# Recurrence of a gated layer: four lanes of image pairs with staggered entry, input scaled in the step's addition, one-step transfers

## The chip, the cores and the metric

The kernel runs on one core of one Trainium2 chip. The metric is device time in microseconds for one execution of the whole program, and the median of several runs is what counts. All data are fp32 in device memory.

## The reference, cut to what matters

The whole network is a 2-D LSTM over 16 images of 64 x 64 tokens with 128 channels, then an attention layer, then a feed-forward layer with a recurrence over the tokens. The change lies in that last part alone:

```python
Wx = einsum('bti,hi->bth', x, W)                    # x: 16 images, 4096 tokens, 128 channels
mean, var = mean(flat), var(flat)                   # over all images and tokens, per channel
Wx = (flat - mean) * rsqrt(var + eps) * gamma + beta
def step(yt, wx_t):
    yt = sigmoid(wx_t + yt @ V.T)
    return yt, yt
_, ys = scan(step, zeros, Wx over the tokens)
t = t + ys
```

The mean and variance need all of Wx, so the recurrence cannot begin before the attention stage has written its last piece of Wx.

## The kernel before, in words

`group_stats`, `lstm_grid`, `landmarks` and `attention` run first. `attention` leaves three things: `wx` in device memory (per image, 128 channels on the partitions by 4096 tokens, before the normalisation), `wx_stats` (its statistics per 512 tokens) and `t2` (the sum that the recurrence's output is added to, tokens by channels).

`recurrence` (L985) works as follows. The 4096 tokens of an image are cut into 128 chunks (CH) of 32 tokens (L). All 128 chunks advance at once, one token per step, so that a step of an image pair (a group, GI = 2) is one tile of 128 channels x 256 columns. Since a chunk does not know the state at its start, 12 warm-up steps (WARM) over the last 12 tokens of the chunk before it produce it; at the end the state so found is compared with the true last state of the chunk before (L1110, L1111), and if any differs too much, `in_order` recomputes everything, which does not happen in the runs shown.

There are eight groups. FLIGHT = 4 of them are in flight together, so there are two rounds (L1097). A round is:

- `begin` (L1031): for each group, four loads of 1 MB of `wx` (L1041) into `rc_w` [channel, 64 chunks, 32 tokens] with three buffers. Each is normalised (x scale + shift) and turned from chunk-major to token-major order on the way, by 16 instructions of 512 columns a group: on GpSimd (POOL, L1050), and in the first round by turns on ScalarE (ACT, L1048). The result, `rc_ws`, holds eight tokens a tile, each as 256 packed columns.
- `warm` (L1064): 12 times over the four groups: a product with V on TensorE (PE, L1061), an addition on VectorE (DVE, L1073) and a sigmoid on ACT (L1074). The first has no product (L1071).
- `step` (L1077): 32 times over the four groups: product, addition in place (L1079), sigmoid in place (L1080).
- `store` (L1083): after each eighth step, for each group: a load of 1 MB of `t2` (L1088), 16 transposes of 128 x 128 on PE (L1093), added into the `t2` tile on DVE by fours (L1094), and a 1 MB store to the output (L1095).

The order on the engines comes from the program's order and a scheduler here; on the queue of SP (SyncE), which issues all the transfers, loads and stores wait for each other's buffers in the order in which they stand. The chunk-major tile, 32 tokens of 4 bytes per chunk, puts one token of neighbouring chunks 128 bytes apart.

Of the kernel before, what the change touches and what calls it, by code (L numbers as in the profile page):

```python
# [8 lines left out]
F32 = mybir.dt.float32  # L9
AF = mybir.ActivationFunctionType  # L10
ALU = mybir.AluOpType
AX = mybir.AxisListType
# [3 lines left out]
P = 128  # L16
# [968 lines left out]
def recurrence(nc, tc, wx, wx_stats, t2, ffn_v, gamma, beta, ident, mhalf, out):  # L985
# [2 lines left out]

    B, H, N = wx.shape
    CH = P
    L = N // CH
    S = 8
    NB = L // S
    GI = 2
    FLIGHT = 4
    WARM = 12
    AGREE = 2.0 ** -18
    NG = B // GI  # L1000
    W = GI * CH
    with ExitStack() as ctx:
        cp = ctx.enter_context(tc.tile_pool(name="rc_c", bufs=1))
        vT = cp.tile([P, P], F32, name="rc_vT")
# [1 line left out]
        shift = cp.tile([P, 1], F32, name="rc_shift")  # L1006
        res = cp.tile([P, NG], F32, name="rc_res")
        with ExitStack() as fast:
            lx = fast.enter_context(tc.tile_pool(name="rc_lx", bufs=3))
            wsp = fast.enter_context(tc.tile_pool(name="rc_wsp", bufs=FLIGHT * NB))  # L1010
            tp = fast.enter_context(tc.tile_pool(name="rc_tp", bufs=4))
            st = fast.enter_context(tc.tile_pool(name="rc_st", bufs=FLIGHT))
            ps_z = fast.enter_context(tc.tile_pool(name="rc_psz", bufs=4, space=PSUM))
            ps_t = fast.enter_context(tc.tile_pool(name="rc_pst", bufs=4, space=PSUM))

            v = cp.tile([P, P], F32, name="rc_v")
            nc.sync.dma_start(out=v, in_=ffn_v)
            vp = ps_t.tile([P, 4, P], F32, tag="t", name="rc_t")
            nc.tensor.transpose(vp[:, 0, :], v, ident)
            nc.vector.tensor_copy(vT, vp[:, 0, :])  # L1020
            mv = cp.tile([P, 2], F32, name="rc_mv")
            nc.vector.bn_aggr(mv, wx_stats.rearrange("p c s -> p (c s)"))
            inv_std(nc, cp, scale, mv[:, 1:2], mhalf, "rc")
            nc.vector.tensor_mul(scale, scale, gamma)
            nc.vector.tensor_mul(shift, mv[:, 0:1], scale)
            nc.vector.tensor_sub(shift, beta, shift)

            class Group:
                pass

            def begin(g):  # L1031
                gr = Group()
                gr.g = g
                gr.ws = [
                    wsp.tile([P, S, GI, CH], F32, tag="ws", name="rc_ws") for _ in range(NB)
                ]
                half = N // 2
                for i in range(GI):
                    for h in range(2):
                        w = lx.tile([P, CH // 2, L], F32, tag="w", name="rc_w")  # L1040
                        nc.sync.dma_start(  # L1041
                            out=w.rearrange("p c l -> p (c l)"), in_=wx[g * GI + i, :, h * half : (h + 1) * half]
                        )
                        for k in reversed(range(NB)):
                            src = w[:, :, k * S : (k + 1) * S].rearrange("p c s -> p s c")
                            dst = gr.ws[k][:, :, i, h * CH // 2 : (h + 1) * CH // 2]
                            if g < FLIGHT and (k + h) % 2:
                                nc.scalar.activation(dst, src, AF.Identity, bias=shift, scale=scale)  # L1048
                            else:
                                nc.gpsimd.tensor_scalar(dst, src, scale, shift, ALU.mult, ALU.add)  # L1050
                gr.a = st.tile([P, GI, CH], F32, tag="a", name="rc_a")
                gr.b = st.tile([P, GI, CH], F32, tag="b", name="rc_b")
                gr.y0 = st.tile([P, GI, CH], F32, tag="y0", name="rc_y0")
                for t in (gr.a, gr.b, gr.y0):
                    nc.vector.memset(t[:, :, 0:1], 0.0)
                gr.last = None
                return gr

            def product(gr):
                z = ps_z.tile([P, GI, CH], F32, tag="z", name="rc_z")  # L1060
                nc.tensor.matmul(z, vT, gr.last, start=True, stop=True)  # L1061
                return z

            def warm(gr, n):  # L1064

                s = L - WARM + n
                w = gr.ws[s // S][:, s % S, :, 0 : CH - 1]
                y = gr.y0 if n == WARM - 1 else (gr.a, gr.b)[n % 2]
                to = y[:, :, 1:CH]
                if gr.last is None:  # L1070
                    nc.scalar.activation(to, w, AF.Sigmoid)  # L1071
                else:
                    nc.vector.tensor_add(to, product(gr)[:, :, 1:CH], w)  # L1073
                    nc.scalar.activation(to, to, AF.Sigmoid)  # L1074
                gr.last = y

            def step(gr, s):  # L1077
                y = gr.ws[s // S][:, s % S]
                nc.vector.tensor_add(y, product(gr), y)  # L1079
                nc.scalar.activation(y, y, AF.Sigmoid)  # L1080
                gr.last = y

            def store(gr, k):  # L1083

                rows = slice(k * S, (k + 1) * S)
                bs = slice(gr.g * GI, (gr.g + 1) * GI)
                tt = tp.tile([P, GI, S, H], F32, tag="tt", name="rc_tt")
                nc.sync.dma_start(out=tt, in_=t2[bs].rearrange("b (c l) f -> c b l f", l=L)[:, :, rows, :])  # L1088
                for s in range(0, S, 2):
                    yp = ps_t.tile([P, GI, 2, P], F32, tag="t", name="rc_t")  # L1090
                    for i in range(GI):
                        for j in range(2):
                            nc.tensor.transpose(yp[:, i, j, :], gr.ws[k][:, s + j, i, :], ident)  # L1093
                    nc.vector.tensor_add(tt[:, :, s : s + 2, :], yp, tt[:, :, s : s + 2, :])  # L1094
                nc.sync.dma_start(out=out[bs].rearrange("b (c l) f -> c b l f", l=L)[:, :, rows, :], in_=tt)  # L1095

            for g0 in range(0, NG, FLIGHT):  # L1097
                groups = [begin(g) for g in range(g0, min(g0 + FLIGHT, NG))]
                for n in range(WARM):
                    for gr in groups:  # L1100
                        warm(gr, n)
                for s in range(L):
                    for gr in groups:
                        step(gr, s)
                    if s % S == S - 1:
                        for gr in groups:
                            store(gr, s // S)
                for gr in groups:
                    d = gr.a[:, :, 1:CH]
                    nc.vector.tensor_sub(d, gr.y0[:, :, 1:CH], gr.last[:, :, 0 : CH - 1])  # L1110
                    nc.vector.tensor_reduce(  # L1111
                        res[:, gr.g : gr.g + 1], d, AX.XY, ALU.max, apply_absolute_value=True
                    )

        worst = cp.tile([P, 1], F32, name="rc_worst")
        nc.vector.tensor_reduce(worst, res, AX.X, ALU.max)
# [121 lines left out]
```

## Time and profile before

| | us |
|---|---|
| median of 3 runs | 4762.01 (4759.21 to 4768.78) |
| the profiled execution's own time | 4758.9 |
| its span, first to last instruction | 4757.4 |
| first load of `rc_w` issued | 4392.8 |
| first sigmoid of the recurrence (L1071) | 4411.3 |
| last state of the first round added (L1079) | 4554.6 |
| first warm-up sigmoid of the last group of round two (L1071) | 4631.4 |
| last state of the second round added (L1079) | 4737.9 |

Over the span the page gives PE 92% busy, DVE 64%, ACT 51% and POOL 56%. These are means over stages with different limits: the first 4390 us are the LSTM and the attention, which the change does not touch. In a line on a group, the columns are the line of the program, the engine, the operation, the tile written and those read, the count, and the shortest, median and longest duration in ns; in a line by stage, they are the stretch in us, then busy time and number of instructions per engine. PEld is PE's loading of weights, which overlaps its products.

### The profile page before, as it was taken

The numbers are of one execution on the slowest core, as the hardware profiler recorded it, in microseconds if no ns is written. First come the engines' busy times: TensorE is split into PE (matmuls) and PEld (weight loads), VectorE is DVE, ScalarE is ACT, GpSimd is POOL, SyncE is SP. The second block draws the span as 40 slices with busy tenths as digits, with TensorE's granted clock in tenths as the row PEclk, the third lists the DMA queues.
The fourth block names the chain that finished last, engine by engine and source line by source line (L and its number), as shares of the span: only waits on it lengthen the run. The fifth ranks groups of instructions, "written<-read, shape, count | busy, mean of one in ns | idle before, by whom it ended". The sixth has DMA issues, their size and how long they took to land. (4 is left out here: it accounts for less than half of the span.)

```text
span 4757.4 us, 102456 instructions
## 1 busy us (share of the span) xinstructions
PE 4368.4 (92%) x39990; PEld 2791.1 (59%) x39990; DVE 3032.8 (64%) x6844; ACT 2438.7 (51%) x4467; POOL 2654.1 (56%) x3587
## 2 busy tenths in 40 slices
PE   7999999999997897899999999999999999986648
PEld 5867655556766894555555555555555555542537
DVE  7777777777776564456665656665566556544549
ACT  0666555556664223455555555555555555532725
POOL 0777777777776000566566656666656666653450
PEclk9999999999997798999999999999999999988769
DMA  7222222323321002122222222222222221111776
GB/s 293 62 76 77 78 76 79 81 78 85 83 70 34 3 14 62 34 56 59 59 57 56 57 63 56 58 58 60 57 57 58 59 58 54 49 47 56 288 295 248
DMA packets 403063, 386.50 MB, mean 81 GB/s; under 512 B 29712, under 2 KB 363408, under 8 KB 396176
## 3 DMA queue, kind: packets, MB, share of 16 engines
q1 hardware_dynamic: 402576, 379.90, 26.1%
q8 instruction: 319, 5.23, 0.5%
q14 instruction: 168, 1.38, 0.1%
HBM read 207.30 MB, written 172.63 MB: 80 GB/s over the span
## 5 line engine op out<-in xcount | busy, mean ns | idle before, releaser
L196 ACT ACTIVATE ls_g<-ls_z,ls_b 128x304 f32<-128x304 f32 (+26 forms) x950 | 508.7, 548 | 370.5 <-PE ls_z L194 334.0
L737 POOL TENSOR_TENSOR at_total<-at_total,at_e 128x512 f32<-128x512 f32 x480 | 610.7, 1272 | 60.5 <-ACT at_e L711 31.6
L190 PE MATMUL ls_z<-ls_xn,ls_w 128*128 128x304 f32 (+26 forms) x1900 | 610.2, 469 | 8.2 <-DMA ls_w<-in_L_conv_wf_dram 5.1
L24 POOL TENSOR_SCALAR at_ve<-at_mu 128x4 f32<-128x4 f32 x128 | 29.3, 229 | 885.4 <-DVE at_mu L866 885.4
L190 PEld LDWEIGHTS ls_z<-ls_xn,ls_w 128*128 128x128 f32 x1900 | 340.8, 196 | 184.5 <-issue 84.0
L668 DVE TENSOR_REDUCE at_mxq<-at_twin 128x2 f32<-128x1024 f32 x256 | 302.2, 1222 | 223.0 <-PE at_twin L664 223.0
L628 POOL TENSOR_SCALAR at_T<-at_T,at_nb 128x128 f32<-128x128 f32 x512 | 400.9, 795 | 13.3
L194 PE MATMUL ls_z<-ls_hsum,ls_u 128*128 128x304 f32 (+26 forms) x1140 | 371.2, 463 | 0.0
L893 ACT COPY at_fx<-at_bank 128x512 f32<-128x512 f32 x128 | 74.9, 585 | 566.8 <-DVE wx_stats L891 368.6
L711 ACT ACTIVATE at_e<-at_twin 128x1024 f32<-128x1024 f32 x256 | 263.5, 1032 | 186.5 <-PE at_twin L703 186.5
L837 DVE STREAM_TRANSPOSE at_dT<-at_twin 128x512 f32<-128x512 f32 x128 | 91.8, 717 | 395.3 <-PE at_twin L834 395.3
L276 POOL TENSOR_TENSOR ls_g<-ls_g,ls_cell 128x304 f32<-128x304 f32 (+26 forms) x190 | 175.9, 926 | 278.7 <-ACT ls_g L196 255.4
L799 DVE TENSOR_REDUCE at_top<-at_twin 128x16 f32<-128x1024 f32 x256 | 310.3, 1212 | 2.0 <-PE at_twin L791 2.0
L194 PEld LDWEIGHTS ls_z<-ls_hsum,ls_u 128*128 128x128 f32 x1140 | 213.4, 196 | 128.6 <-issue 78.2
L876 ACT ACTIVATE at_z<-at_u,at_nb,at_r 128x128 f32<-128x128 f32 x512 | 210.8, 482 | 135.3 <-POOL at_nb L871 135.2
L823 ACT ACTIVATE at_eT<-at_twin 128x1024 f32<-128x1024 f32 x256 | 247.7, 1019 | 52.2 <-PE at_twin L818 52.1
L233 ACT ACTIVATE ls_tt<-ls_tt,ls_nb 128x128 f32<-128x128 f32 (+9 forms) x632 | 261.0, 478 | 4.1 <-POOL ls_nb L228 4.1
L194 PE MATMUL ls_z<-ls_h,ls_u 128*128 128x304 f32 (+26 forms) x760 | 259.6, 465 | 2.3 <-DVE ls_h L284 2.1
L224 POOL TENSOR_TENSOR ls_tt<-ls_ve,mhalf 128x4 f32<-128x4 f32 (+2 forms) x190 | 228.7, 1203 | 15.2
L277 DVE TENSOR_TENSOR ls_g<-ls_g,ls_g 128x304 f32<-128x304 f32 (+26 forms) x190 | 98.4, 518 | 194.4 <-POOL ls_g L276 193.2
L225 POOL TENSOR_TENSOR ls_tt<-ls_ve,mhalf 128x4 f32<-128x4 f32 (+2 forms) x190 | 214.5, 1129 | 0.0
L194 PEld LDWEIGHTS ls_z<-ls_h,ls_u 128*128 128x128 f32 x760 | 142.4, 196 | 91.4 <-issue 50.9
(242 smaller groups left out, 10213.1 us busy)
## 6 DMA issues: line engine op xcount, KB each, us to landing
t<-ls_tt SPq DMA_DIRECT2D x392, 130.0 KB
at_T<-t SPq DMA_DIRECT2D x128, 264.0 KB
gs_xb<-in_x_dram SPq DMA_DIRECT2D x16, 2048.0 KB
at_xh<-t SPq DMA_DIRECT2D x128, 256.0 KB
t<-at_u SPq DMA_DIRECT2D x128, 256.0 KB
wx<-at_fx SPq DMA_DIRECT2D x128, 256.0 KB
rc_w<-wx SPq DMA_DIRECT2D x32, 1024.0 KB
rc_tt<-t SPq DMA_DIRECT2D x32, 1024.0 KB
```

What stands on the lines that cost most here:

```text
L190: nc.tensor.matmul(v.z[g][:, : v.cols], wt[g], v.xn, start=True, stop=False)
L194: nc.tensor.matmul(view(v, v.z[g]), ut[g], hin, start=False, stop=True)
L196: nc.scalar.activation(a[:, : v.cols], v.z[g][:, : v.cols], AF.Tanh if g == 4 else AF.Sigmoid, bias=bt[g])
L224: nc.gpsimd.tensor_tensor(v.tt[:, 0:k, F + 2], ve[:, 0, :k], mhalf[:, :k], ALU.pow)
L225: nc.gpsimd.tensor_tensor(v.tt[:, 0:k, F + 3], ve[:, 1, :k], mhalf[:, :k], ALU.pow)
L233: nc.scalar.activation(v.tt[:q, k, F + 4 :], v.tt[:q, k, 0:F], AF.Identity, bias=v.nb[:q, k : k + 1], scale=v.tt[:q, k, F + 3 : F + 4],)
L628: nc.gpsimd.tensor_scalar(x[:, c, :], x[:, c, :], nb[:, 0, c : c + 1], nb[:, 1, c : c + 1], ALU.mult, ALU.subtract)
L668: nc.vector.tensor_reduce(gr.im.mxq[:, 2 * i : 2 * i + 2, gr.g], s[i], AX.X, ALU.max)
L711: nc.scalar.activation(gr.e[:, 2 * i : 2 * i + 2].rearrange("p n c m -> p (n c m)"), gr.s[i].rearrange("p n m -> p (n m)"), AF.Exp)
L737: nc.gpsimd.tensor_tensor(total, total, e[:, :, c, :], ALU.add)
L799: nc.vector.tensor_reduce(gr.top[:, 2 * i : 2 * i + 2, 0:2, :].rearrange("p n j c -> p n c j"), gr.s[i].rearrange("p n (c j m) -> p n c j ...
L823: nc.scalar.activation(gr.eT[:, 2 * i : 2 * i + 2].rearrange("p n t -> p (n t)"), s[i].rearrange("p n t -> p (n t)"), AF.Exp)
```

## The change

`recurrence` alone is changed.

- The two rounds become four lanes. Lane g takes group g and then group g + 4; it enters nine steps (APART) after the lane before it, and its second group starts 45 steps after its first. The loop runs over 117 time slots. In each slot every live lane first issues its product, then its addition and sigmoid, then its transposes, in an order written out by hand for PE, DVE, ACT and POOL.
- The tile `rc_w` [channel, image, chunk, 32 tokens] holds a whole group, five such tiles exist, and the states overwrite the inputs in place. There is no token-major copy: the addition, the sigmoid, the product and the transposes of a main step all read or write columns that lie 128 bytes apart. Warm-up states still go to packed tiles, while their inputs are read from `rc_w`.
- The scaling moves into the step: the addition is a scalar_tensor_tensor (input x scale + product) with `scale` as a per-channel pointer, and the shift becomes the sigmoid's bias, a pointer as well. POOL has no work in the steps.
- `wx` comes in eight pieces of 512 KB a group, one a slot (the first two groups at once, in slot 0). `t2` and the output move in pieces of four steps, 512 KB each, with 2 KB runs in device memory (4 KB before); a `t2` piece is asked for three slots ahead of its first step. Each pair of steps is turned and added as soon as it is done.

```diff
@@ -988,17 +988,22 @@
 
 
 
+
+
     B, H, N = wx.shape
     CH = P
     L = N // CH
-    S = 8
+    S = 4
+    AHEAD = 3
     NB = L // S
     GI = 2
-    FLIGHT = 4
+    LANES = 4
+    PARTS = 8
     WARM = 12
     AGREE = 2.0 ** -18
     NG = B // GI
-    W = GI * CH
+    STEPS = WARM + L
+    APART = 9
     with ExitStack() as ctx:
         cp = ctx.enter_context(tc.tile_pool(name="rc_c", bufs=1))
         vT = cp.tile([P, P], F32, name="rc_vT")
@@ -1006,10 +1011,9 @@
         shift = cp.tile([P, 1], F32, name="rc_shift")
         res = cp.tile([P, NG], F32, name="rc_res")
         with ExitStack() as fast:
-            lx = fast.enter_context(tc.tile_pool(name="rc_lx", bufs=3))
-            wsp = fast.enter_context(tc.tile_pool(name="rc_wsp", bufs=FLIGHT * NB))
-            tp = fast.enter_context(tc.tile_pool(name="rc_tp", bufs=4))
-            st = fast.enter_context(tc.tile_pool(name="rc_st", bufs=FLIGHT))
+            wp = fast.enter_context(tc.tile_pool(name="rc_wp", bufs=LANES + 1))
+            tp = fast.enter_context(tc.tile_pool(name="rc_tp", bufs=8))
+            st = fast.enter_context(tc.tile_pool(name="rc_st", bufs=2))
             ps_z = fast.enter_context(tc.tile_pool(name="rc_psz", bufs=4, space=PSUM))
             ps_t = fast.enter_context(tc.tile_pool(name="rc_pst", bufs=4, space=PSUM))
 
@@ -1028,89 +1032,105 @@
             class Group:
                 pass
 
-            def begin(g):
+            def place(g):
                 gr = Group()
                 gr.g = g
-                gr.ws = [
-                    wsp.tile([P, S, GI, CH], F32, tag="ws", name="rc_ws") for _ in range(NB)
-                ]
-                half = N // 2
-                for i in range(GI):
-                    for h in range(2):
-                        w = lx.tile([P, CH // 2, L], F32, tag="w", name="rc_w")
-                        nc.sync.dma_start(
-                            out=w.rearrange("p c l -> p (c l)"), in_=wx[g * GI + i, :, h * half : (h + 1) * half]
-                        )
-                        for k in reversed(range(NB)):
-                            src = w[:, :, k * S : (k + 1) * S].rearrange("p c s -> p s c")
-                            dst = gr.ws[k][:, :, i, h * CH // 2 : (h + 1) * CH // 2]
-                            if g < FLIGHT and (k + h) % 2:
-                                nc.scalar.activation(dst, src, AF.Identity, bias=shift, scale=scale)
-                            else:
-                                nc.gpsimd.tensor_scalar(dst, src, scale, shift, ALU.mult, ALU.add)
+                gr.images = slice(g * GI, (g + 1) * GI)
+                gr.w = wp.tile([P, GI, CH, L], F32, tag="w", name="rc_w")
+                gr.tt = {}
+                return gr
+
+            def load_part(gr, n):
+                i, k = divmod(n, PARTS // GI)
+                part = slice(k * N * GI // PARTS, (k + 1) * N * GI // PARTS)
+                nc.sync.dma_start(out=gr.w[:, i].rearrange("p c l -> p (c l)")[:, part], in_=wx[gr.g * GI + i, :, part])
+
+            def rows(a, gr, k):
+                return a[gr.images].rearrange("b (c l) f -> c b l f", l=L)[:, :, k * S : (k + 1) * S, :]
+
+            def load_sum(gr, k):
+                gr.tt[k] = tp.tile([P, GI, S, H], F32, tag="tt", name="rc_tt")
+                nc.sync.dma_start(out=gr.tt[k], in_=rows(t2, gr, k))
+
+            def begin(gr):
                 gr.a = st.tile([P, GI, CH], F32, tag="a", name="rc_a")
                 gr.b = st.tile([P, GI, CH], F32, tag="b", name="rc_b")
-                gr.y0 = st.tile([P, GI, CH], F32, tag="y0", name="rc_y0")
+                gr.y0 = st.tile([P, GI, CH], F32, tag="y0", name="rc_y0", bufs=LANES)
                 for t in (gr.a, gr.b, gr.y0):
                     nc.vector.memset(t[:, :, 0:1], 0.0)
                 gr.last = None
-                return gr
 
             def product(gr):
-                z = ps_z.tile([P, GI, CH], F32, tag="z", name="rc_z")
-                nc.tensor.matmul(z, vT, gr.last, start=True, stop=True)
-                return z
-
-            def warm(gr, n):
-
-                s = L - WARM + n
-                w = gr.ws[s // S][:, s % S, :, 0 : CH - 1]
-                y = gr.y0 if n == WARM - 1 else (gr.a, gr.b)[n % 2]
-                to = y[:, :, 1:CH]
-                if gr.last is None:
-                    nc.scalar.activation(to, w, AF.Sigmoid)
+                gr.z = None
+                if gr.last is not None:
+                    gr.z = ps_z.tile([P, GI, CH], F32, tag="z", name="rc_z")
+                    nc.tensor.matmul(gr.z, vT, gr.last, start=True, stop=True)
+
+            def state(gr, n):
+
+
+                if n < WARM:
+                    w, z = gr.w[:, :, 0 : CH - 1, L - WARM + n], slice(1, CH)
+                    gr.last = gr.y0 if n == WARM - 1 else (gr.a, gr.b)[n % 2]
+                    y = gr.last[:, :, 1:CH]
                 else:
-                    nc.vector.tensor_add(to, product(gr)[:, :, 1:CH], w)
-                    nc.scalar.activation(to, to, AF.Sigmoid)
-                gr.last = y
-
-            def step(gr, s):
-                y = gr.ws[s // S][:, s % S]
-                nc.vector.tensor_add(y, product(gr), y)
-                nc.scalar.activation(y, y, AF.Sigmoid)
-                gr.last = y
-
-            def store(gr, k):
-
-                rows = slice(k * S, (k + 1) * S)
-                bs = slice(gr.g * GI, (gr.g + 1) * GI)
-                tt = tp.tile([P, GI, S, H], F32, tag="tt", name="rc_tt")
-                nc.sync.dma_start(out=tt, in_=t2[bs].rearrange("b (c l) f -> c b l f", l=L)[:, :, rows, :])
-                for s in range(0, S, 2):
-                    yp = ps_t.tile([P, GI, 2, P], F32, tag="t", name="rc_t")
-                    for i in range(GI):
-                        for j in range(2):
-                            nc.tensor.transpose(yp[:, i, j, :], gr.ws[k][:, s + j, i, :], ident)
-                    nc.vector.tensor_add(tt[:, :, s : s + 2, :], yp, tt[:, :, s : s + 2, :])
-                nc.sync.dma_start(out=out[bs].rearrange("b (c l) f -> c b l f", l=L)[:, :, rows, :], in_=tt)
-
-            for g0 in range(0, NG, FLIGHT):
-                groups = [begin(g) for g in range(g0, min(g0 + FLIGHT, NG))]
-                for n in range(WARM):
-                    for gr in groups:
-                        warm(gr, n)
-                for s in range(L):
-                    for gr in groups:
-                        step(gr, s)
-                    if s % S == S - 1:
-                        for gr in groups:
-                            store(gr, s // S)
-                for gr in groups:
-                    d = gr.a[:, :, 1:CH]
-                    nc.vector.tensor_sub(d, gr.y0[:, :, 1:CH], gr.last[:, :, 0 : CH - 1])
-                    nc.vector.tensor_reduce(
-                        res[:, gr.g : gr.g + 1], d, AX.XY, ALU.max, apply_absolute_value=True
-                    )
+                    w, z = gr.w[:, :, :, n - WARM], slice(0, CH)
+                    gr.last = y = w
+                if gr.z is None:
+                    nc.scalar.activation(y, w, AF.Sigmoid, bias=shift, scale=scale)
+                else:
+                    nc.vector.scalar_tensor_tensor(y, w, scale, gr.z[:, :, z], ALU.mult, ALU.add)
+                    nc.scalar.activation(y, y, AF.Sigmoid, bias=shift)
+
+            def turn(gr, s):
+
+                yp = ps_t.tile([P, GI, 2, P], F32, tag="t", name="rc_t")
+                for i in range(GI):
+                    for j in range(2):
+                        nc.tensor.transpose(yp[:, i, j, :], gr.w[:, i, :, s + j], ident)
+                k, r = divmod(s, S)
+                tt = gr.tt[k][:, :, r : r + 2, :]
+                nc.vector.tensor_add(tt, yp, tt)
+                if r == S - 2:
+                    nc.sync.dma_start(out=rows(out, gr, k), in_=gr.tt[k])
+
+            def check(gr):
+                d = st.tile([P, GI, CH - 1], F32, tag="d", name="rc_d", bufs=1)
+                nc.vector.tensor_sub(d, gr.y0[:, :, 1:CH], gr.last[:, :, 0 : CH - 1])
+                nc.vector.tensor_reduce(res[:, gr.g : gr.g + 1], d, AX.XY, ALU.max, apply_absolute_value=True)
+
+
+            starts = [APART * (g % LANES) + (STEPS + 1) * (g // LANES) for g in range(NG)]
+
+            due = [starts[g - LANES - 1] + STEPS + 1 if g > LANES else starts[g] - 2 * APART for g in range(NG)]
+            groups = {}
+            with tc.manual_schedule(
+                engines={mybir.EngineType.PE, mybir.EngineType.DVE, mybir.EngineType.Activation, mybir.EngineType.Pool}
+            ):
+                for t in range(max(starts) + STEPS + 1):
+                    for g in range(NG):
+                        if t == max(due[g], 0):
+                            groups[g] = place(g)
+                        for n in range(PARTS):
+                            if t == max(due[g] + n, 0):
+                                load_part(groups[g], n)
+                    live = [(groups[g], t - starts[g]) for g in range(NG) if 0 <= t - starts[g] <= STEPS]
+                    for gr, n in live:
+                        if n == 0:
+                            begin(gr)
+                        if n < STEPS:
+                            product(gr)
+                    for gr, n in live:
+                        if n < STEPS:
+                            state(gr, n)
+                    for gr, n in live:
+                        s = n - WARM
+                        if s + AHEAD >= 0 and (s + AHEAD) % S == 0 and (s + AHEAD) // S < NB:
+                            load_sum(gr, (s + AHEAD) // S)
+                        if s > 0 and s % 2 == 0:
+                            turn(gr, s - 2)
+                        if n == STEPS:
+                            check(gr)
 
         worst = cp.tile([P, 1], F32, name="rc_worst")
         nc.vector.tensor_reduce(worst, res, AX.X, ALU.max)
```

## The prediction

> **What bounds the kernel now.** The page's table of 40 slices shows that only the last three or four slices, the recurrence, load the DMA engines, so I asked for the busy time by stage of that stretch (columns: length, busy us and instructions of PE, PEld, DVE, ACT, POOL, then granted PE clock, DMA share, GB/s).
>
> ```profile
> 4396.00:4411.00 15.00, 0.00 (x0) 0.00 (x0) 2.11 (x17) 10.52 (x9) 11.03 (x11) 0.50 1.00 390
> 4411.00:4446.00 35.00, 3.66 (x6) 1.51 (x6) 1.27 (x3) 30.51 (x32) 27.59 (x24) 0.50 0.95 357
> 4480.00:4565.00 85.00, 76.68 (x453) 65.13 (x451) 80.30 (x167) 41.03 (x101) 14.67 (x12) 0.96 0.85 329
> 4565.00:4632.00 67.00, 3.78 (x7) 1.63 (x7) 3.34 (x17) 2.90 (x7) 59.15 (x51) 0.50 0.78 276
> 4653.00:4748.00 95.00, 86.98 (x508) 73.28 (x506) 91.69 (x193) 52.50 (x129) 0.00 (x0) 0.98 0.76 293
> ```
>
> The recurrence takes 361 of 4757.4 us. Some 117 us of it (15 + 35 + 67) are input staging: PE and DVE idle while data land and POOL and ACT scale them. The two rounds proper are bound by DVE (80.3 of 85, 91.7 of 95 us) with PE close behind. The chain that ended last agrees: in the gap between the rounds it runs through the POOL scaling.
>
> ```profile
> 4592.74 17.93 POOL rc_ws L1050 x16
> 4611.45 19.94 POOL rc_ws L1050 x17
> 4631.88 34.07 PE rc_z L1061 x146
> ```
>
> The prices come from the answers for single lines (count, then shortest/median/longest ns), and three of them are about *spacing*, which the change turns on:
>
> ```profile
> L1079 DVE TENSOR_TENSOR rc_ws<-rc_z,rc_ws x256: 415/425/426, 4467.6 to 4737.9; 128x256 f32<-128x256 f32 x128
> L1080 ACT ACTIVATE rc_ws<-rc_ws x256: 416/417/422, 4468.1 to 4738.3; 128x256 f32<-128x256 f32 x128
> L1094 DVE TENSOR_TENSOR rc_tt<-rc_t,rc_tt x128: 680/681/692, 4481.5 to 4747.2; 128x512 f32<-128x512 f32 x128
> L1048 ACT ACTIVATE rc_ws<-rc_w,rc_shift,rc_scale x32: 1234/1247/1263, 4399.2 to 4444.8; 128x512 f32<-128x512 f32 x32
> L376 ACT ACTIVATE kl<-lm_bank x2: 1042/1048/1055, 1509.5 to 1510.6; 128x512 f32<-128x512 f32 x2
> L893 ACT COPY at_fx<-at_bank x128: 585/585/587, 2010.4 to 4393.5; 128x512 f32<-128x512 f32 x128
> L807 PEld LDWEIGHTS at_bank<-ident,at_top x512: 195/212/370, 1979.5 to 4367.1; 128*128 128x128 f32 x171
> L849 PEld LDWEIGHTS at_twin<-ident,at_R x512: 137/141/144, 1992.6 to 4380.8; 128*128 128x128 f32 x171
> L681 DVE TENSOR_TENSOR at_split<-at_mx,at_split x16: 167/959/962, 1889.0 to 4093.1; 128x4 f32<-128x4 f32 x16
> L1024 DVE TENSOR_TENSOR rc_scale<-rc_scale,ffn_gamma x1: 159/159/159, 4398.1 to 4398.1; 128x1 f32<-128x1 f32 x1
> L446 DVE TENSOR_SCALAR lm_z<-lm_xt,lm_zscale x8: 478/479/486, 1590.5 to 1691.4; 128x512 f32<-128x512 f32 x8
> L384 DVE TENSOR_SCALAR lm_eye<-lm_eye x3: 419/420/420, 1503.7 to 1504.4; 128x512 f32<-128x512 f32 x3
> ```
>
> L376 writes 512 elements 256 bytes apart in 1048 ns; L893 writes them packed in 585: 0.9 ns more per element, twice the packed rate of 0.83. Those are the same 128 partitions and the same engine.
>
> **What the Trainium skill says.** *Advanced Engine Details and Errata*, § SBUF Cachelines: SBUF has 16-byte lines, and an access that goes to another line each time is penalised. The trace agrees for ACT (above), and for PE's weight load at 16-byte spacing (L807, 212 against 141 ns). *ScalarE: Activation LUTs*, § Rules for kernel authors: about 0.3 us + 0.83 ns per element with a bias pointer. In the trace, L196 (bias pointer, PSUM source) takes 513 ns for 304 and 687 for 512 columns, which is 259 + 0.835 n; agreed. *VectorE: DVE Perf Modes*, § The TRN2 errata: an fp32 tensor_tensor costs (N+151)/0.96 ns, 424 for N = 256; L1079 has 425. *TensorE: Matmul & The Clock Gate*, Part 1: without activity PE runs at half clock; the stages above show 0.50 when PE is idle.
>
> **Part by part.**
>
> *Removed: the scaling.* 96 POOL instructions x 1.197 = 115 us and 32 ACT ones x 1.247 = 40 us, with the 67 us between the rounds and most of the 35 us start-up. The new order keeps up to four lanes running across groups.
>
> *Moved into the step.* The input stays [image, chunk, step], so one step's 256 elements now lie 32 x 4 = 128 bytes apart for everything that touches them.
> - ACT: sigmoid in place, spaced, with bias pointer. 417 ns less 256 x 0.83 leaves 204; a pointer adds about 100 (L196's 259 against 158 left of L893's 585). So 0.30 + 256 x 1.7 = 0.74 us for the 32 main steps and 0.52 for the 12 warm ones, which write a packed tile.
> - DVE: the addition becomes scalar_tensor_tensor with a pointer. L446 less L384 puts the pointer at 60 ns: 0.485 if spacing is free. If DVE also halves, its fixed 0.158 + 0.06 + 256 x 2.08 = 0.75. No long spaced DVE access is in this trace; the one hint is L681, four elements, two operands spaced: 167 ns, where 159 (one element, L1024) and 175 (16 elements, L67) put four packed ones at 163. Four ns more for four elements is one more cycle each, so I take 0.75, in warm steps too, which read the spaced input. Bounds 0.485 and 0.75.
> - PE: a packed product takes 0.43 us (eight passes, 1.89 us, start 0.216 apart). With spacing from nothing to double: 0.43 to 0.86. A transpose's weights are spaced now: 32 of L1093 take 3.84 us, some 0.115 each; four of L807 start 0.12 to 0.15 apart. I take 0.45 and 0.125, since L807's loads start nearly as fast as packed ones though each lasts longer.
>
> *The steady slot.* A lane repeats every 45 slots: 43 additions, 16 turn additions (L1094), 0.76 us of check. Four lanes, per slot:
> - DVE (43 x 0.75 + 16 x 0.681 + 0.76) x 4/45 = 3.90 us
> - ACT (12 x 0.52 + 32 x 0.74) x 4/45 = 2.66 us
> - PE (12 x 0.43 + 31 x 0.45 + 64 x 0.125) x 4/45 = 2.4 us
>
> DVE sets it; ACT's and PE's increases lie beside DVE.
>
> *The ramps.* Starts nine slots apart give 117 slots: nine each with one, two and three lanes, 62 with about four, and 28 on the way down. One lane is a loop: addition 0.75, sigmoid 0.52, product until DVE may read it 0.65 (half clock 1.3), semaphores 0.1: 2.0 to 2.7. So up: 21 + 22 + 25 us; middle: 62 x 3.90 = 242; down: 9 x 3.27 = 29 (DVE, three lanes with turns), 24, 26. Sum 389 us.
>
> *Transfers.* The same 100.7 MB in 512 KB pieces. At the 350 GB/s of the stages above that is 288 us, under 389, so I cost the smaller pieces at nothing; that cover is gone below some 300 us. On SP's queue an output store waits for its last turn addition, and the loads behind it wait too; loads are queued three slots early (used five after), over 10 us against the few that a piece takes, so nothing shows. If loads came late, the turn addition would hold DVE, and all lanes with it.
>
> *Start and end.* The first load now waits for all of attention's memory (five tiles fill the pool), so it follows the last wx store of 4394.15, about 2 us on; 4.2 MB at 390 GB/s are 10.8 us: first sigmoid near 4409.5 (4411.25 before). From the last check to the end it took 7 us before; the same.
>
> Sum: 4409.5 + 389 + 7 = 4805.5 against the span of 4757.4: +48 us. The profiled execution took 4758.9 (1.5 around the span); the median of the runs is 4762.0, so 4810.
>
> **The rivals.** (1) *DVE reads spaced data at full rate.* For it: L681's four ns are thin evidence, and DVE's packed element is the slowest already (1.04 ns in L1079, ACT's 0.83), so a given delay would show least there. Against: ACT shows the halving cleanly in both directions. Then the slot is (43 x 0.485 + 10.9 + 0.76) x 4/45 = 2.89, the middle 182, ramps 56 and 65: 303 us, end 4720, time 4724: faster. Each 0.1 us on the addition is worth about 34 us, so it decides below about 0.61 us.
> (2) *PE's moving operand halves*: a product of 0.86 makes PE (5.2 + 26.7 + 8) x 4/45 = 3.54 a slot; with a cheap DVE some 362 us, time 4783; with DVE also slow about 4825, and with transposes of 0.2 us too, 4850. For: the skill's cachelines. Against: L807's spacing of starts.
> (3) *Half way*: a spaced DVE element at ACT's 1.7 ns: addition 0.65, time about 4775.
>
> **How the numbers follow.** Forecast 0.55 (4795 to 4850, slow PE included), rival 1 0.22, rival 2 with a fast DVE 0.13, rival 3 0.10. A measurement tells about 0.2%, 9.5 us, from none. Rival 1 gives nearly all of faster, 0.23; the overlap of 1 and 3 near 4762 is 0.07; slower 0.70. The range 4735 to 4850 leaves out most of rival 1 (0.15) and the worst of PE (0.05). Since both signs have weight: the forecast's own range is 4795 to 4850.
>
> **What would show it.** The group of the new addition at about 750 ns and the sigmoid at 740 (main) and 520 (warm); DVE over 90% busy in the four-lane stretch, slots of 3.9 us; no POOL work; DMA near 255 GB/s. An addition near 490 ns and a slot under 3.2 us would prove it wrong; so would PE busy with starts 0.43 apart per pass, or long DVE waits for rc_tt loads.

## The result and the profile after

The changed kernel takes 4799.81 us, the median of four runs (4795.85 to 4811.63), against 4761.16 us for the kernel before on the same chip. The ratio is 1.0082 with a 95% interval of 1.0061 to 1.0103: slower by some 39 us. The profiled execution of the changed kernel took 4795.85 us and its span is 4794.3 us, 36.9 us longer than the span of before.

All of it lies in the recurrence. Its first sigmoid starts at 4408.75 us (4411.25 before), so 2.5 us were gained ahead of it, and from there to the end it takes 385.6 us (346.2 before). The staging stretches in which PE and DVE stood idle are gone, as the change meant, and more than their time came back in the steps. The view by stage of the changed kernel shows where. Its columns are the stretch and its length, busy us and instructions of PE, PEld, DVE, ACT and POOL, the granted PE clock, the DMA share and GB/s.

```profile
4440.00:4490.00 50.00, 44.24 (x150) 26.68 (x149) 38.51 (x67) 30.78 (x50) 0.00 (x0) 0.91 0.47 154
4490.00:4570.00 80.00, 80.00 (x303) 48.55 (x302) 74.46 (x123) 59.78 (x86) 0.00 (x0) 1.00 0.84 297
4570.00:4640.00 70.00, 68.25 (x262) 42.36 (x261) 66.05 (x114) 51.11 (x79) 0.00 (x0) 1.00 0.94 325
4640.00:4740.00 100.00, 97.44 (x364) 58.05 (x363) 91.90 (x150) 71.27 (x99) 0.00 (x0) 1.00 0.70 236
```

POOL has no work, as forecast. But with four lanes running (from about 4482 to 4706 us) PE is the fullest engine, and in the 80 us from 4490 it has no gap: 80.00 of 80 us. DVE is close behind at 74.5, and a reader who looks at DVE alone takes it for the bound: it is busy 93% of the time. The chain that ended last decides between them. From 4482 to 4569 us and from 4646 to 4706 it never leaves PE:

```profile
4528.13 3.45 PE rc_z L1067 x8
4531.58 0.88 PE rc_t L1090 x8
4532.47 3.46 PE rc_z L1067 x8
4535.92 0.89 PE rc_t L1090 x8
4536.82 3.45 PE rc_z L1067 x8
4540.27 0.89 PE rc_t L1090 x8
```

Between those two stretches, where the second groups enter, the chain passes at times over DVE and ACT and once over a load of `t2`; PE has 85% of it over the whole of the four lanes. Eight passes of products (four lanes, two passes each) in 3.45 us are 0.43 us a pass, twice the 0.216 us of the kernel before. Eight transposes in 0.89 us are 0.111 us each, where packed ones started 0.109 us apart in the kernel before. The answers for single lines (count, then shortest/median/longest ns) carry the prices:

```profile
L1067 PE MATMUL rc_z<-rc_w,rc_vT x496: 589/610/796, 4439.3 to 4783.0; 128*128 128x256 f32 x166
L1067 PE MATMUL rc_z<-rc_a,rc_vT x96: 377/379/796, 4409.7 to 4680.3; 128*128 128x256 f32 x96
L1090 PEld LDWEIGHTS rc_t<-ident,rc_w x512: 185/189/231, 4443.6 to 4785.5; 128*128 128x128 f32 x171
L1082 DVE SCALAR_TENSOR_TENSOR rc_w<-rc_w,rc_scale,rc_z x256: 632/702/898, 4437.8 to 4783.7; 128x256 f32<-128x256 f32 x128
L1083 ACT ACTIVATE rc_w<-rc_w,rc_shift x256: 735/784/992, 4438.5 to 4784.4; 128x256 f32<-128x256 f32 x128
L1083 ACT ACTIVATE rc_b<-rc_b,rc_shift x40: 489/504/541, 4411.6 to 4674.4; 128x254 f32<-128x254 f32 x40
L1093 DVE TENSOR_TENSOR rc_tt<-rc_t,rc_tt x128: 665/681/748, 4445.1 to 4786.2; 128x512 f32<-128x512 f32 x128
```

The first two are the same line of the program, the same weights and the same shape: the warm steps read a packed state (379 ns), the main steps a spaced one (610). The starts of the lanes' first sigmoids (L1080) and of their checks (L1099) cut the recurrence into the prediction's parts: slots 0 to 27 take 73.7 us, 27 to 89 take 223.8 (3.61 a slot), 89 to 116 take 80.6, and 7.5 are left to the end.

### The profile page after: what moved, and what is told of

It reads as the page before. It is cut to its first block, busy times and chain, and to the rows that moved or that the text cites. A ratio compares the mean times of both kernels' runs of the same rounds, so it can differ in the third digit from the quotient of the medians.

```text
span 4794.3 us, 102460 instructions
## 1 busy us (share of the span) xinstructions
PE 4481.3 (93%) x39990; PEld 2806.2 (59%) x39990; DVE 3112.5 (65%) x6844; ACT 2498.4 (52%) x4435; POOL 2544.8 (53%) x3491
## 5 line engine op out<-in xcount | busy, mean ns | idle before, releaser
L1067 PE MATMUL rc_z<-rc_w,rc_vT 128*128 128x256 f32 x496 | 237.8, 619 | 22.4 <-ACT rc_w L1083 22.0
L1083 ACT ACTIVATE rc_w<-rc_w,rc_shift 128x256 f32<-128x256 f32 x256 | 198.1, 797 | 115.4 <-DVE rc_w L1082 110.9
L224 POOL TENSOR_TENSOR ls_tt<-ls_ve,mhalf 128x4 f32<-128x4 f32 (+2 forms) x190 | 228.6, 1203 | 15.2
```

Source lines behind the costliest of these rows:

```text
L1067: nc.tensor.matmul(gr.z, vT, gr.last, start=True, stop=True)
L1083: nc.scalar.activation(y, y, AF.Sigmoid, bias=shift)
```

## The experiments

Two theories stood against each other. *PE's moving operand* (B in the expectations): the product that reads columns 128 bytes apart runs at half rate and sets the slot; DVE would be second, at 3.0 us or less. (The moving operand is here the state that the product reads; V is loaded as weights.) *DVE's addition* (C): as in the forecast, DVE sets the slot, and PE's busy time is only long because its records are. Theory A lies between: both engines are slowed and level, at some 3.45 us. All ratios are to the kernel before. Slots are counted as above.

**A control for room.** The tiles of the next experiments need memory, which comes out of the `t2` buffers.

```diff
-    AHEAD = 3
+    AHEAD = 1
...
-            tp = fast.enter_context(tc.tile_pool(name="rc_tp", bufs=8))
+            tp = fast.enter_context(tc.tile_pool(name="rc_tp", bufs=6))
```

> Control for the packed-state runs, which need SBUF: the changed kernel with six t2 tiles in place of eight, asked for one slot ahead in place of three. All theories: as the changed kernel, 4800 us within 8; a longer time would say that the lead of the transfers carries some of its cost.

Measured: 4798.53 us, ratio 1.0078 [1.0061, 1.0095]; the four-lane stretch again takes 223.8 us. Eight buffers in place of six, and asking for `t2` three slots ahead, rather than one, carry nothing here, and the experiments below, which all have this edit, can be compared with the changed kernel.

**A packed state for the product and the transposes.** The addition still works in place on spaced columns; the sigmoid writes a packed tile, which the product and the transposes read.

```diff
-                    gr.last = y = w
+                    gr.last = y = gr.ys[n - WARM] = packed()
...
-                    nc.vector.scalar_tensor_tensor(y, w, scale, gr.z[:, :, z], ALU.mult, ALU.add)
-                    nc.scalar.activation(y, y, AF.Sigmoid, bias=shift)
+                    d = y if n < WARM else w
+                    nc.vector.scalar_tensor_tensor(d, w, scale, gr.z[:, :, z], ALU.mult, ALU.add)
+                    nc.scalar.activation(y, d, AF.Sigmoid, bias=shift)
...
-                        nc.tensor.transpose(yp[:, i, j, :], gr.w[:, i, :, s + j], ident)
+                        nc.tensor.transpose(yp[:, i, j, :], gr.ys[s + j][:, i, :], ident)
```

> As the control, but the sigmoid writes a packed tile, which product and transposes read; the addition still works in place on spaced columns. Theory A (PE at 3.48 us a slot and DVE at 3.45 are level, each engine loses half its rate at 128-byte spacing): PE falls to 2.3 a slot, DVE stays, the four-lane middle gains only some 5 to 10 us and the ramps 10 to 15 by the shorter product: about 4778. Theory B (PE's spaced product alone sets the slot): the middle falls to 3.0 us a slot or less, about 4745. Theory C (DVE's spaced addition alone sets it): the middle does not move, about 4785.

Measured: 4757.97 us, ratio 0.9992 [0.9983, 1.0001]: some 40 us of the loss are gone, though the addition works on the same spaced columns and the sigmoid, which still reads them, takes 728 ns (784 in the changed kernel). The four-lane stretch takes 199.0 us (3.21 a slot). That meets none of the three theories in size: the middle gained 24.8 us, where A gave 5 to 10 and C nothing, and B had DVE at 3.0 us or less and a time of 4745. First the view by stage, then the chain:

```profile
4480.00:4560.00 80.00, 72.53 (x345) 46.73 (x345) 79.97 (x135) 59.77 (x99) 1.77 (x18) 1.00 0.90 306
```

```profile
4496.98 1.20 DVE rc_tt L1095 x2
4498.18 1.77 DVE rc_w L1084 x3
4499.95 0.55 DVE rc_p L1084
```

Now DVE has no gap (79.97 of 80 us) and holds the chain. So DVE's own load, with the spaced addition, is 3.21 us a slot and not 3.9. The chain shows why: three spaced additions take 1.77 us, 0.59 each, and two turn additions 1.20, 0.60 each, while the answers for these lines have medians of 704 and 684 ns. One instruction starts about 0.1 us before the record of the one ahead ends. Over 4485 to 4640 us the medians from start to start are 0.615 us for a spaced addition after another, 0.56 for a warm one and 0.60 for a turn addition, and with these DVE needs (11 x 0.56 + 32 x 0.615 + 16 x 0.60 + 0.76) x 4/45 = 3.22 us a slot, where 3.21 were measured.

**A cheap addition with the spaced product.** The reverse: the addition reads a fixed packed tile of zeros and writes a packed one; the sigmoid still writes the spaced state and the product reads it. The input is left out of the recurrence here.

```diff
-                    nc.vector.scalar_tensor_tensor(y, w, scale, gr.z[:, :, z], ALU.mult, ALU.add)
-                    nc.scalar.activation(y, y, AF.Sigmoid, bias=shift)
+                    d = st.tile([P, GI, CH], F32, tag="f", name="rc_f", bufs=6)[:, :, z]
+                    nc.vector.scalar_tensor_tensor(d, fixed[:, :, z], scale, gr.z[:, :, z], ALU.mult, ALU.add)
+                    nc.scalar.activation(y, d, AF.Sigmoid, bias=shift)
```

> As the control, but the addition reads a packed tile of zeros in place of the input and writes a packed tile, and the sigmoid still writes spaced columns, which product and transposes read. It leaves the input out of the recurrence. The addition falls from 0.70 to about 0.48 us. Theory A and B: PE holds the slot at 3.48, 5 to 15 us gained in all, about 4788. Theory C: the slot falls to 2.7 us, about 4740.

Measured: 4775.33 us, ratio 1.0028 [1.0018, 1.0038]. Some 13 us of what it gains on the control lie ahead of the steps: the first sigmoid, which here waits for no load, comes at 4396.9 us, not 4410.3. With the start of the control it would be near 4789, as A and B had it. The four-lane stretch takes 220.6 us (3.56 a slot), though the addition fell from 702 to 480 ns:

```profile
4480.00:4560.00 80.00, 80.00 (x306) 48.86 (x305) 61.38 (x123) 55.02 (x85) 0.00 (x0) 1.00 0.82 288
```

DVE drops from 93% to 77% busy and the slot hardly moves; PE keeps all of its 80 us. The additions now mostly start 0.86 us apart, which is two passes of 0.433: each waits for its product. A third of the addition's time is worth 3 us of 224 in this stretch. That excludes the theory of DVE's addition.

**Spacing by itself.** A program with none of the network and with constant data measures the four instructions alone, each in runs of eight calls (sixteen of the transposes), with their spaced operand's elements 4, 8, 16, 32, 64 and 128 bytes apart.

```diff
+        for _ in range(8):
+            nc.tensor.matmul(z()[:, 0:256], ident, at(big, 32), start=True, stop=True)
...
+        for _ in range(16):
+            nc.tensor.transpose(z()[:, 0:128], at(big, 32, 128), ident)
...
+        for _ in range(8):
+            nc.vector.scalar_tensor_tensor(d(), at(big, 16), s, zz[:, 0:256], ALU.mult, ALU.add)
```

> Prices by themselves: products of 256 columns, weight loads of 128, sigmoids and additions of 256 elements on tiles whose elements lie 4, 8, 16, 32, 64 or 128 bytes apart, with none of the network's work (it leaves all of it out). Theory A: at 128 bytes PE's pass goes from 0.216 to 0.43 us, ACT's element from 0.83 to 1.67 ns and DVE's by a similar amount, and the step comes where neighbours no longer share a 16-byte line, so 16 bytes cost as much as 128. Rival: the cost grows with the spacing, and 16 bytes are nearly free, as the transposes' loads at 16 bytes suggested.

The answers for single lines, with first and last start after the durations: L67, L69, L71 and L77 are products with 4, 8, 16 and 128 bytes between columns; L79, L81, L83 and L89 the weight loads of transposes with 4, 8, 16 and 128; L91, L95 and L101 sigmoids reading at 4, 16 and 128 bytes; L109, L111 and L113 additions reading at 4, 8 and 16, and L121 reading and writing at 16.

```profile
L67 PE MATMUL z<-big,ident x16: 379/379/379, 30.8 to 34.0; 128*128 128x256 f32 x16
L69 PE MATMUL z<-big,ident x16: 386/387/390, 34.2 to 37.6; 128*128 128x256 f32 x16
L71 PE MATMUL z<-big,ident x16: 609/632/632, 37.9 to 44.6; 128*128 128x256 f32 x16
L77 PE MATMUL z<-big,ident x16: 608/610/611, 59.4 to 65.9; 128*128 128x256 f32 x16
L79 PEld LDWEIGHTS z<-ident,big x16: 139/141/160, 65.9 to 67.8; 128*128 128x128 f32 x16
L81 PEld LDWEIGHTS z<-ident,big x16: 195/209/209, 68.0 to 69.7; 128*128 128x128 f32 x16
L83 PEld LDWEIGHTS z<-ident,big x16: 210/213/214, 69.9 to 71.7; 128*128 128x128 f32 x16
L89 PEld LDWEIGHTS z<-ident,big x16: 192/193/194, 75.4 to 77.1; 128*128 128x128 f32 x16
L91 ACT ACTIVATE d<-big,s x8: 492/492/509, 9.5 to 12.3; 128x256 f32<-128x256 f32 x8
L95 ACT ACTIVATE d<-big,s x8: 735/740/751, 16.0 to 20.5; 128x256 f32<-128x256 f32 x8
L101 ACT ACTIVATE d<-big,s x8: 713/720/735, 31.3 to 35.7; 128x256 f32<-128x256 f32 x8
L109 DVE SCALAR_TENSOR_TENSOR d<-big,s,zz x8: 474/474/480, 51.0 to 53.7; 128x256 f32<-128x256 f32 x8
L111 DVE SCALAR_TENSOR_TENSOR d<-big,s,zz x8: 474/474/474, 54.1 to 56.9; 128x256 f32<-128x256 f32 x8
L113 DVE SCALAR_TENSOR_TENSOR d<-big,s,zz x8: 678/684/722, 57.2 to 61.5; 128x256 f32<-128x256 f32 x8
L121 DVE SCALAR_TENSOR_TENSOR to<-big,s,zz x8: 662/667/735, 76.9 to 81.9; 128x256 f32<-128x256 f32 x8
```

For what PE's product, ACT and DVE read, the step lies between 8 and 16 bytes, and no more is lost in going on to 128. The passes of the product start 0.216 us apart at 4 bytes, 0.225 at 8, 0.453 at 16 and 0.433 at 128 (medians of fifteen intervals): the last is the pass of the changed kernel. A weight load's record grows from 141 to 193 ns at 128 bytes, but its starts lie 0.109 and 0.112 us apart, and 0.122 at 16 bytes. A record that is a third longer and starts that are hardly farther apart: this is what misled the prediction. The weight load also has no step where the others have it, since its record is as long at 8 bytes as at 16 (209 and 213 ns). The Trainium skill, *Advanced Engine Details and Errata*, § SBUF Cachelines, says that a 16-byte line needs at least two hits to hide the memory's latency; two fp32 elements 8 bytes apart are two hits, 16 bytes apart are one, and for the product, the sigmoid and the addition the runs agree in both.

**All states packed.** The addition, too, writes a packed tile; only its input is still read from spaced columns.

```diff
-                    gr.last = y = w
+                    gr.last = y = gr.ys[n - WARM] = packed()
...
-                        nc.tensor.transpose(yp[:, i, j, :], gr.w[:, i, :, s + j], ident)
+                        nc.tensor.transpose(yp[:, i, j, :], gr.ys[s + j][:, i, :], ident)
```

> As the control, but the addition writes a packed tile, and sigmoid, product and transposes work on it; only the addition's input is read at 128-byte spacing. Sigmoid 0.50, product 0.43, addition 0.63 us, as the warm steps have them. Theory A: DVE sets the slot at 3.3 us; the middle gains 19 us and the ramps about 20 (0.7 us off each loop): about 4757. Theory B: PE no longer matters, slot at most 3.0, about 4740. Theory C: 3.3 us a slot as in A.

Measured: 4745.57 us, ratio 0.9965 [0.9953, 0.9978], faster than both kernels and between A's 4757 and B's 4740. The parts are 65.1, 192.2 (3.10 a slot) and 63.3 us.

```profile
4480.00:4560.00 80.00, 72.13 (x354) 47.80 (x352) 79.93 (x142) 50.14 (x99) 2.19 (x23) 1.00 0.92 327
```

DVE is full, as in the first version with a packed state; ACT fell from 59.8 to 50.1 us, since its sigmoid is packed again. The gain on that version is 12 us by the medians. The two profiled executions lie further apart, by 21.5 us, and of these 6.8 are in the middle and 12.7 on the ramps, where few lanes run and each waits for its own product, addition and sigmoid in turn.

**The lanes with no spacing at all.** The scaled token-major copy is put back, by pieces, on POOL (half of the first group's on ACT); the additions and sigmoids are those of the kernel before.

```diff
+                src, dst = x.rearrange("p (c l) -> p l c", l=L), gr.w[:, :, i, k * CH * GI // PARTS : (k + 1) * CH * GI // PARTS]
+                if gr.g == 0 and n % 2:
+                    nc.scalar.activation(dst, src, AF.Identity, bias=shift, scale=scale)
+                else:
+                    nc.gpsimd.tensor_scalar(dst, src, scale, shift, ALU.mult, ALU.add)
...
-                    nc.vector.scalar_tensor_tensor(y, w, scale, gr.z[:, :, z], ALU.mult, ALU.add)
-                    nc.scalar.activation(y, y, AF.Sigmoid, bias=shift)
+                    nc.vector.tensor_add(y, gr.z[:, :, z], w)
+                    nc.scalar.activation(y, y, AF.Sigmoid)
```

> The four lanes, with the token-major scaled copy of the kernel before put back: each piece of the input is scaled and turned on its way (POOL, half of the first group on ACT), and every step reads and writes packed columns, with the plain addition of 0.425 us and the sigmoid of 0.417 us. If the spacing alone makes the changed kernel slow, the four-lane slot is DVE's (43 x 0.425 + 16 x 0.68 + 0.76) x 4/45 = 2.66 us or PE's (43 x 0.43 + 64 x 0.12) x 4/45 = 2.33, while the transfers at some 350 GB/s want about 2.9: slots of 2.7 to 3.0 us over steps 27 to 89, near 180 us, and a time near 4720, below both kernels. POOL has 64 copies of some 2.4 us, 154 us in all, beside the rest. Rival, the order in lanes itself costs (few lanes on the ramps, loads waiting for their copies): not below 4762, with slots over 3.2 us or a start over 20 us later.

Measured: 4740.23 us, ratio 0.9959 [0.9946, 0.9973]. So the order in lanes, with its small pieces, is worth about 20 us, and the spaced columns, together with the scaling in the step that came with them, cost the changed kernel some 59. The two were not taken apart here. The expected 4720 was missed. Slots 72 to 89, when all input is in, run at 2.45 us a slot, better than expected, with PE and DVE both full (4650 to 4670 us below). Slots 45 to 72, while the input of three groups arrives, took 100.1 us (3.71 a slot), with neither full:

```profile
4560.00:4640.00 80.00, 61.00 (x286) 50.39 (x287) 52.98 (x128) 34.17 (x92) 38.28 (x18) 0.85 0.93 318
4650.00:4670.00 20.00, 20.00 (x124) 18.02 (x122) 19.94 (x47) 11.54 (x33) 0.00 (x0) 1.00 0.82 269
```

```profile
4562.45 5.98 DMA rc_x<-wx
...
4568.62 2.14 POOL rc_w L1056
...
4570.78 4.33 DMA rc_x<-wx
...
4575.20 2.18 POOL rc_w L1056
```

There the chain goes from load to copy to load. Only two staging buffers of 512 KB fit: with four, 9 KB a partition were still wanted and 1.34 were left.

**Half pieces.** To tell a shortage of buffers from one of transfer, the same room was cut into four buffers of half the size.

```diff
-    PARTS = 8
+    PARTS = 16
...
-            lx = fast.enter_context(tc.tile_pool(name="rc_lx", bufs=2))
+            lx = fast.enter_context(tc.tile_pool(name="rc_lx", bufs=4))
```

> The lanes with the packed, scaled copy, its input now in 16 pieces of 256 KB a group and four staging buffers of half the size, which fill the same room. Before, steps 45 to 72 took 3.3 to 4.1 us a slot while the input of groups 5 to 7 came in, and 72 to 89, with none, 2.45. If the two staging buffers set that (a load of some 5.2 us and a copy of 2.1, two at a time: 3.65 us a piece and slot), four half pieces at a time give two pieces in some 2 x (4.5 + 1.1) / 4 = 2.8 us: slots of 2.8 to 3.1 there, some 15 to 20 us less, a time near 4722. Rival, the DMA engines themselves: they are 93 to 98% busy in that stretch at 318 to 344 GB/s, so smaller pieces leave the slots at 3.3 to 4.1 us and the time within 5 us of 4740 or above.

Measured: 4743.66 us, ratio 0.9959 [0.9946, 0.9972]: no gain. Slots 45 to 72 went from 100.1 to 93.0 us, against the 75 to 84 that the buffers alone would give; the first sigmoid came 8.5 us later, and slots 9 to 18 took 33.0 us in place of 18.6. The first two groups are staged in the `t2` buffers, of which a half piece fills only half, so less was under way at the start; that this is the cause was not shown. In the stretch at issue the DMA engines are busy nearly throughout:

```profile
4560.00:4640.00 80.00, 57.52 (x294) 47.90 (x293) 54.68 (x133) 33.34 (x91) 53.03 (x43) 0.95 0.98 349
```

The shortage of buffers is not the whole of it; the share of 0.98 speaks for the transfers, but that a faster transfer would help was not tried.

**Lanes six steps apart.** The version with packed states, with shorter ramps.

```diff
-    APART = 9
+    APART = 6
...
-                            if t == max(due[g] + n, 0):
+                            if t == max(due[g] + n * APART // PARTS, 0):
```

> The kernel with the packed states, with lanes that enter six steps apart in place of nine (and the input pieces asked for faster to match). If its middle is DVE's, 3.1 us a slot, and its ramps cost 2.4 us a slot with less than four lanes, then 108 slots in place of 117 give 18 x 2.4 + 72 x 3.1 + 18 x 2.35 = 309 us in place of 320.6: a time about 11 us less, near 4735. Rival, the transfers: the same 100.7 MB in 309 us are 326 GB/s, near what the stretches above reach, and loads come late: no gain, with DVE below 95% busy in the middle and waits for rc_w or rc_tt in the chain.

Measured: 4748.06 us, ratio 0.9976 [0.9966, 0.9986], no better than nine apart. The ramps shrank as expected, from 65.1 to 43.8 us up and from 63.3 to 48.1 down, but the 71 slots between them took 234.9 us, not 220. The six slots from 45 on took 26.1 us, 4.35 each, and there the chain runs through transfers:

```profile
4539.78 6.08 DMA out_dram<-rc_tt
...
4545.89 6.95 DMA rc_tt<-t
```

A store of the output and a load into the same buffer behind it hold the turn addition and with it DVE. From 4545 to 4575 us the DMA engines are full:

```profile
4545.00:4575.00 30.00, 21.02 (x84) 15.47 (x83) 22.54 (x39) 13.45 (x27) 1.01 (x10) 0.83 1.02 383
```

The rival held: what the ramps give, the transfers take. Whether more `t2` buffers, or a longer lead, would have covered that wait was not tried.

## Why the prediction was right, and where it was wrong

The sign, the size and the range hold: 4799.8 against 4810, within 4735 to 4850 and within the forecast's own 4795 to 4850. The mechanism does not, and that the number came out is luck.

*The step that failed* is the price of the product: "I take 0.45 and 0.125, since L807's loads start nearly as fast as packed ones though each lasts longer." The 0.125 was right to 0.014 us. The 0.45 was 0.865, the upper bound that the prediction itself named. L807 is a weight load and was made the witness for the moving operand; the spacing program shows that the two differ, with a pass at twice its interval and a weight load at nearly the same one (0.112 against 0.109 us). Nor does L807's longer record show the 16-byte lines, as the prediction read it, since the record is as long at 8 bytes. With the measured prices PE needs (12 x 0.43 + 31 x 0.865 + 64 x 0.111) x 4/45 = 3.47 us a slot, and 3.61 were measured over slots 27 to 89. Those hold more main steps than a lane's whole cycle does on the mean (slots 27 to 44 took 3.68 each), and where the second groups enter the chain leaves PE for a while. "PE's moving operand halves", which the prediction gave as its second rival, is what happened.

*DVE's 3.90 us a slot* was too much, for two reasons. The addition took 0.70 us, not 0.75: a spaced element costs less than twice a packed one (684 less 474 ns over 256 elements is 0.8 ns more, on 1.04). And instructions in a row start closer together than their records are long, 0.615 us for the addition and 0.60 for the turn addition. With a packed product, DVE fills 3.21 us a slot. The sum over recorded durations counted about 0.1 us for each of 59 instructions that DVE doesn't spend.

The same reading stood at the start of the prediction, where the two rounds are called DVE's because it is busy 80.3 of 85 us. In the main steps of the kernel before, the additions start 0.432 us apart (median), which is two passes of its product at 0.216; only the turn additions go at DVE's own pace. In the lanes with no spacing, where the chain stays on DVE for a while, packed additions start 0.33 us apart, though their records are 0.41 us long. The chain shows both, 98 passes of the product in 21.17 us before the change, and four additions in 1.33 us in those lanes:

```profile
4459.82 21.17 PE rc_z L1061 x98
```

```profile
4656.11 1.33 DVE rc_w L1092 x4
```

So the forecast was held up by two errors of opposite sign: DVE's load was 0.7 us a slot too high, PE's 1.1 too low, and the larger of the two true values, 3.61, is near the 3.90 taken. In the middle this gave 223.8 us in place of 242.

*ACT*, forecast 0.74 and 0.52, took 0.784 and 0.504 us: right, and beside other work (59.8 of 80 us busy). *The ramps*, forecast 68 and 79, took 73.7 and 80.6. The first nine slots on the way down, priced at 29 us by DVE, took 29.7, but by luck as well: the same slots took 29.1 with the cheap addition and 25.6 with the packed product, so PE set them. *The start*, forecast 4409.5, came at 4408.75 by other terms: the last store of `wx` went out at 4391.24 and not at 4394.15, the first load 2.3 us later as said, and from there it took 15.2 us. The prediction's own terms give 4407. *The end*, forecast 7, took 7.5. *Transfers at nothing*: right for the changed kernel. Its chain does show one wait for a `t2` piece:

```profile
4634.54 5.94 DMA rc_tt<-t
```

But the control, which has no such wait in the chain there, needs as long for slots 63 to 72 (31.4 against 31.3 us). That cover is not deep: in the two versions that need the input sooner, with staging buffers or six steps apart, transfers do end up in the chain.

*The first rival*, spaced reads at full rate on DVE, fell: the addition is 702 ns, and by starts 0.615 us against 0.39 packed (L109). Two of its sums were slightly off, with no effect: the middle is 62 x 2.89 = 179 us, not 182, and its four packed elements come to 162 ns, not 163. The time given for a slow PE with a fast DVE, 4783, fits the experiment that makes just that: 4775 with a start 13.4 us earlier. *The third rival*, 1.7 ns a spaced element on DVE, was near the mark (1.04 and 0.8 are 1.86 by the records), but DVE did not set the slot.

## What to carry to other kernels

Price a strided operand by its role, from a row with the same role: here a matmul's moving operand lost half its rate when neighbouring columns were 16 bytes or more apart (a pass in 0.43 to 0.46 us, 0.216 packed), and a transpose that loads such columns as weights lost little (0.11 to 0.12 us, 0.109 packed). If a layout has to stay spaced in memory, let the instruction that must read it write a packed result, so that the penalty is paid once and not by every reader after it: that turned 39 us lost into 16 gained. And take an engine's load from starts, not from durations, wherever its instructions follow each other without a gap.

## What the runs showed of the hardware

- For reads the penalty is a step, not a slope: between 8 and 16 bytes, then flat to 128 within a tenth, on PE's moving operand (starts 0.225, 0.453 and 0.433 us apart at 8, 16 and 128 bytes), ACT (records of 740 and 720 ns at 16 and 128, 492 packed) and DVE (684 ns at 16, 648 at 128, 474 packed).
- Writing to spaced columns as well costs DVE a little more, which the records hide. At 16 bytes they are 667 against 684 ns, but L121's starts lie 0.70 us apart and L113's 0.61. All calls of L121 write one tile, so a wait may be in that; in the lanes the addition in place started every 0.615 us, the one that only reads spaced columns every 0.57.
- A weight load from columns 128 bytes apart has a record a third longer (193 against 141 ns) at nearly the same interval of starts, 0.112 against 0.109 us.
- Two instructions of DVE in a row overlap in the records by some 0.08 to 0.1 us: the turn additions last 0.68 us and start 0.60 apart.
